# Graph attention on one core: two slots of layer 0 per loop pass, scores in one burst, PSUM banks shared out anew

## The chip, the cores and the metric

The kernel runs on one core of a Trainium2 chip. The metric is device time in microseconds from the first to the last instruction of a launch, with what little lies around it; the shown figure is the median of three runs. Engines are named as the profile names them: PE (TensorE, matrix products; PEld its weight loads), DVE (VectorE), ACT (ScalarE), POOL (GpSimd) and SP (SyncE, which issues most transfers). Products land in PSUM[...].

## The reference

Input is `x` (8 batches, 2048 nodes, 256 features) and a symmetric 0/1 matrix `adj` (2048 x 2048) with ones on the diagonal. Layer 0 is masked attention with 4 heads of 64, with a softmax of its own over every chunk of 256 keys; the chunks' contexts are added up.

```python
scores = jnp.einsum('bhnd,bhjcd->bhnjc', q, kc) / jnp.sqrt(64)
scores = jnp.clip(scores, -10.0, 10.0)
scores = jnp.where(mask == 0, -10.0, scores)
attn = jax.nn.softmax(scores, axis=-1)              # over the 256 keys of a chunk
ctx = jnp.einsum('bhnjc,bhjcd->bhnd', attn, vc)     # summed over the 8 chunks
out = layernorm(ctx @ Wo.T + bo + x) * gamma + beta
x = layernorm(x + out)
```

Layer 1 is a graph attention on the result:

```python
Wh = (x @ W)                                        # 4 heads of 64
e = leaky_relu(s_src[i] + s_dst[j], 0.2), -inf where adj == 0
alpha = softmax(e over j);  h = elu(alpha @ Wh)
x = layernorm(x + h)
```

All of it is float32.

## The kernel before

Layer 0 of a batch runs as 64 slots. A slot is one block of 512 query nodes (`q`, four of them), one pair of heads (`hp`, two) and one chunk of 256 keys (`c`, eight); 16 slots make a group, one block of queries. `scores` (L367) computes for a slot two tiles of 128 keys by 2 heads by 512 queries. Each tile takes two PSUM banks from `two_banks` (L102), which alternates between two such pairs. DVE clips each tile against a mask slab and writes it to SBUF as `pr` (L388, 1024 elements per partition); ACT takes the exponential in place (L400). `product` (L402), once per head, multiplies 512 queries' weights with the values and a column of ones (32 records of a 64-wide weight), and ACT copies the result from the one bank `pc` of the pool `psC` to `raw` (L419). `normalize` (L421) takes DVE's reciprocal of the sums (L427), and POOL scales and adds up (L434, L436).

Layer 1 of the batch before runs beside it. Its work is 192 tiles per batch: 12 units (4 heads for each of three blocks of 6, 5 and 5 tiles of 128 nodes), 16 tiles of source nodes each. `make` (L699) lets DVE form a tile `e` of edge weights (L712, 768 or 640 elements per partition; four buffers), `use` (L723) multiplies it into one bank `pa` that stays open over the unit's 16 tiles (L732). The pool `psL` has two such banks, so the next unit can begin in the other. `close` (L749) is a generator that finishes a unit in steps, one step at each call of `rest`: reciprocals of the sums read from the bank, scaling on ACT, exponential and relu, and the sum into `h1`.

Every engine runs its queue in program order; the order below is written out by hand. In slot `s` the loop of L901 emits: the slab load of slot s+3; the reciprocal of slot s-1; the scores and clips of slot s+1; the step of other work that belongs to this slot; the first product of slot s; the exponentials of slot s+1; three tiles of layer 1 (`lower.step`); the second product of slot s; and other work behind it. Three tiles of layer 1 are made ahead at the start of a batch.

The other work is kept in tables by slot number within a group. `BESIDE` holds DVE's parts of finishing the previous group (output bias, sums, statistics of the layer norms, a transpose), `BEHIND` and `AFTER` those of PE and ACT (output product, values of layer 1); small PSUM tiles for them come from one bank of the pool `psM`. In the first group of batches 2 to 7 there is no previous group, and `CLOSING` has the final norm of layer 1 of batch b-2 instead. Batch 0 has no layer 1 beside it. In its slots `masks.step` (L210) turns the matrix `adj` into the stored slabs and edges instead: a PE transpose, a DVE pass and an ACT copy per piece, through `psL`. Without layer 1 the second product of a slot uses `psL`, so that the two products have a bank each; the last batch's final slots, which have no layer 1 either (`LATE`), use the one bank. Between batches stand the projections of the next batch and the last group's steps. After batch 7 layer 1 runs alone.

PSUM in all: two pairs for `two_banks`, one bank `psC`, two `psL`, one `psM`.

Of the kernel before, what the change touches and what calls it, by code (L numbers as in the profile page):

```python
# [22 lines left out]
def adj_resnorm_kernel(  # L23
# [45 lines left out]
    LATE = 14  # L69
    WIDE = max(BANKS)  # L70
    JG = 4
    assert TILES == STEP * SLOTS and NT % JG == 0

    consts = ctx.enter_context(tc.tile_pool(name="consts", bufs=1))
    big = ctx.enter_context(tc.tile_pool(name="big", bufs=1))
    prp = ctx.enter_context(tc.tile_pool(name="prp", bufs=4))
    ep = ctx.enter_context(tc.tile_pool(name="ep", bufs=4))
    slabs = ctx.enter_context(tc.tile_pool(name="slabs", bufs=4))
    edges = ctx.enter_context(tc.tile_pool(name="edges", bufs=3))
# [4 lines left out]
    psL = ctx.enter_context(tc.tile_pool(name="psL", bufs=2, space=bass.MemoryType.PSUM))  # L84
    psM = ctx.enter_context(tc.tile_pool(name="psM", bufs=1, space=bass.MemoryType.PSUM))
# [16 lines left out]
    def two_banks(shape, name):  # L102

        turn_of[0] ^= 1
        return psA.tile(shape, F32, tag=f"psA{turn_of[0]}", name=name)
# [57 lines left out]
    def finish_constants():  # L163
        for k, a_sb in enumerate(aa):
            for c in range(KC):
                wa = small.tile([P, F], F32, tag="ee", name="wa")
                nc.vector.tensor_mul(wa, w1_sb[:, c, :F], a_sb)
                nc.vector.tensor_reduce(
                    w1_sb[:, c, F + k * H : F + (k + 1) * H],
                    wa.rearrange("p (h d) -> p h d", h=H),  # L170
                    AX.X,
                    ALU.add,
                )


        pb0 = psM.tile([P, CH], F32, tag="psM", name="pb0")
        for c in range(KC):
            nc.tensor.matmul(
                pb0[:, :F],
                lhsT=bv_sb[:, c : c + 1].to_broadcast([P, P]),  # L180
                rhs=wo_sb[:, c, :],
                start=(c == 0),
                stop=(c == KC - 1),
            )
        nc.vector.scalar_tensor_tensor(
            bo_sb, pb0[:, :F], float(NK), bo_sb, op0=ALU.mult, op1=ALU.add
        )

        nc.vector.tensor_sub(beta_sb, beta_sb, bo_sb)

# [8 lines left out]
    class Masks:  # L199
# [34 lines left out]
        def turn(self, t, m, ab):  # L234
            n, j0 = BANKS[m], FIRST[m]
            pm = psL.tile([P, WIDE, P], BF16, tag="psL", name="pm")
# [61 lines left out]
    def project(b, g):  # L298
# [14 lines left out]
        def linear(dst, w, bias, apart=False):  # L313
            if apart:
                pps = [psL.tile([P, CH], F32, tag="psL", name="pp") for _ in range(KC)]
            else:
                pp = two_banks([P, KC, CH], "pp")
                pps = [pp[:, c, :] for c in range(KC)]
            for c in range(KC):
                for kc in range(KC):  # L320
                    nc.tensor.matmul(  # L321
                        pps[c],
                        lhsT=w[:, kc, c * P : (c + 1) * P],
                        rhs=st["xT"][:, kc, :],
                        start=(kc == 0),
                        stop=(kc == KC - 1),
                    )
            for c in range(KC):
                nc.scalar.activation(  # L329
                    dst[:, c, cols], pps[c], AF.Identity, bias=bias[:, c : c + 1]  # L330
                )

        def values():
# [20 lines left out]
            lambda: linear(qT, wq_sb, bq_sb, b > 0 and g == NCH - 1),  # L354
# [11 lines left out]

    def scores(s):  # L367
        q, hp, c = where[s]
        slab = slab_of.pop(s)
        cols = slice(q * CH, (q + 1) * CH)  # L370
        pss = []
        for u in range(KT):
# [11 lines left out]
            pss.append(ps)  # L384
        probs[s] = []
# [70 lines left out]
    def context(q, hp):  # L456
        acc = accs.pop((q, hp))
        pt = psM.tile([P, CH], F32, tag="psM", name="pt")
# [42 lines left out]
    class Between:  # L501
# [3 lines left out]
        def __init__(self, b, g, sd, waug):  # L505
            self.b, self.g, self.sd, self.waug = b, g, sd, waug
            self.r = load_x(b, g, "xg")
            self.y = blocks.tile([P, QT, F], F32, tag="y", name="y")
# [9 lines left out]
        def output(self, us):  # L518
# [3 lines left out]
            else:  # L522
                po = psM.tile([P, 2, F], F32, tag="psM", name="po")
# [39 lines left out]
        def values(self, us):  # L563
            n, t = len(us), QT * self.g + us[0]
            if n == 1:
                pw = psM.tile([P, 1, CH], F32, tag="psM", name="pw")
# [22 lines left out]
    AHEAD = {12: lambda o: o.load()}  # L589
    BESIDE = {  # L590
        1: [lambda o: o.bias()],
        4: [lambda o: o.add((0, 1))],
        5: [lambda o: o.add((2, 3)), lambda o: o.a.stats((0, 1))],
# [4 lines left out]
        14: [lambda o: o.turn()],  # L598
    }
    BEHIND = {  # L600
        3: lambda o: o.output((0, 1)),
        4: lambda o: o.output((2, 3)),
        7: lambda o: o.a.apply(o.y),
        11: lambda o: o.finish(),
        14: lambda o: o.values((0,)),
        15: lambda o: o.values((1,)),
    }

    BESIDE_0 = {i: steps for i, steps in BESIDE.items() if i != 14} | {15: BESIDE[14]}
    BEHIND_0 = {i: step for i, step in BEHIND.items() if i != 14} | {15: BEHIND[14]}  # L610
    AFTER_0 = {i: lambda o, i=i: o.values((i + 1,)) for i in range(3)}
    AFTER = {0: lambda o: o.values((2,)), 1: lambda o: o.values((3,))}

    def factors(b, sd, waug):
# [10 lines left out]
        def most():  # L625
            nc.vector.tensor_reduce(top, d, AX.X, ALU.max)
            pt = psM.tile([P, CH], F32, tag="psM", name="pt")
# [4 lines left out]
        def spread():  # L632
            pb = psM.tile([P, CH], F32, tag="psM", name="pb")
# [16 lines left out]
        def rows():  # L650

            pr = psM.tile([P, CH], F32, tag="psM", name="pr1")
# [15 lines left out]
    class Layer1:  # L668
# [54 lines left out]
        def use(self):  # L723
# [17 lines left out]
            if j == NT - 1:  # L741
                self.tail.append(self.close(n, self.pa))

# [5 lines left out]
        def close(self, u, pa):  # L749
            m, h = UNITS[u]  # L750
            n = BANKS[m]
            pav = pa[:, : n * D1].rearrange("p (k d) -> p k d", k=n)

            dn = small.tile([P, n, 1], F32, tag="dn", name="dn")
            nc.vector.tensor_scalar(dn, pav[:, :, D:D1], 1e-30, None, ALU.max)  # L755
            nc.vector.reciprocal(dn, dn)  # L756
            yield 1
            hh = small.tile([P, n, D], F32, tag="hh", name="hh")
            for k in range(n):
                nc.scalar.activation(hh[:, k, :], pav[:, k, :D], AF.Copy, scale=dn[:, k, :])  # L760
# [3 lines left out]
            nc.scalar.activation(ee, hh, AF.Exp)  # L764
            hp = small.tile([P, n, D], F32, tag="hp", name="hp")
            nc.scalar.activation(hp, hh, AF.Relu)  # L766
# [8 lines left out]
            )  # L775

# [6 lines left out]
    class Close:  # L783
# [12 lines left out]
        def finish(self):  # L796
            o = blocks.tile([P, QT, F], F32, tag="y", name="o")
            self.n.apply(o)
            outgoing.append(lambda: nc.sync.dma_start(out=by_node(out, self.b, self.g), in_=o))
# [26 lines left out]
    for g in range(NCH):  # L826
# [10 lines left out]
        masks.step()  # L837
        if g == 1:
# [9 lines left out]
        3: [(1, "add"), (2, "load")],  # L848
        4: [(1, "stats")],
# [13 lines left out]
        4: [(0, "finish"), (2, "load")],  # L863
        5: [(1, "finish"), (3, "load")],
# [19 lines left out]
    for b in range(B):  # L884
        waug = blocks.tile([P, NT, H, D1], F32, tag="waug", name="waug")
        sd = small.tile([P, 2 * H, NT], F32, tag="sd", name="sd", bufs=1)
        if b == 0:
            for s in range(3):
                load_slab(s)
            scores(0)  # L890
            for u in range(KT):
                exps(0, u)
        if lower:
            for _ in range(STEP):
# [5 lines left out]
        beside, behind, after = (BESIDE, BEHIND, AFTER) if b else (BESIDE_0, BEHIND_0, AFTER_0)  # L900
        for s in range(SLOTS):  # L901
            q, hp, c = where[s]
            i = s % QS
            send()
            if s + 3 < SLOTS:
                load_slab(s + 3)
            if i == 0:
                before = group
                group = Between(b, q - 1, sd, waug) if q else None
            if i == 1 and q:  # L910
# [3 lines left out]
            if group and i in AHEAD:  # L914
                AHEAD[i](group)
            if s == SLOTS - 3 and b + 1 < B:
                turns = [project(b + 1, g) for g in range(NCH)]
                turns[0].pop(0)()
            if s:
                normalize(s - 1)  # L920
            if s + 1 < SLOTS:
                scores(s + 1)

            if s == SLOTS - 1 and b + 1 < B:
                turns[0].pop(0)()
            if i == 3 and q:
                turn_context(q - 1, 1)
            if i == QS // 2 + 3:
                turn_context(q, 0)
            if group:  # L930
                for step in beside.get(i, ()):
                    step(group)
            elif closing:
                closing.do(s, behind=False)
            product(s, 0, not lower)
            if s + 1 < SLOTS:
                for u in range(KT):
                    exps(s + 1, u)
            if lower:
                if b + 1 < B or s < SLOTS - LATE:  # L940
                    lower.step()
            elif masks.left():
                masks.step()
            product(s, 1, not lower)

            if before and i in after:
                after[i](before)
            if i == 0 and q:
                send_context(b, q - 1, 1)
            if i == QS // 2:  # L950
                send_context(b, q, 0)
            if group and i in behind:
                behind[i](group)
            elif closing and not q:
                closing.do(s, beside=False)
# [6 lines left out]
        every = tuple(range(QT))  # L962
# [20 lines left out]
        if b + 1 < B:  # L983
            (k0, v0, q0), (l1, t1, k1, v1, q1), (l2, t2, k2, v2, q2), (l3, t3, k3, v3, q3) = turns
            rest = [lambda: lower.rest(1)] if lower else []
            first = [] if b else [lambda: before.values((1,))]
            order = [begin, *rest, l1, *rest, *first, lambda: before.values((2, 3))]
            order += [*rest, ctx, *rest, k0]
            order += [steps[0], t1, steps[1], v0, steps[2], steps[3], l2, k1, steps[4], q0]
            order += [steps[5], v1, t2, l3, steps[6], q1, steps[7], k2, steps[8], steps[9], t3, v2]  # L990
            order += [lambda: [load_slab(s) for s in range(3)], fs[0], q2, fs[1], k3, fs[2], v3]
            order += [lambda: scores(0), q3, lambda: [exps(0, u) for u in range(KT)]]
        else:
# [5 lines left out]
            order += [step, lambda: lower.rest(4)]  # L999
# [62 lines left out]
```

## Time and profile before

| | us |
|---|---|
| three runs, median | 3833.12 (3832.3 to 3833.25) |
| the profiled execution | 3836.74 |
| its span, first to last instruction | 3835.0 |
| PE busy in the span | 3696.8 |
| DVE busy | 3203.6 |
| ACT busy | 1950.1 |
| slots of batch 0 (64.74 to 384.70) | 319.96 |
| 16 slots beside units of 5 tiles (2032.39 to 2133.28) | 100.89 |
| 16 slots beside units of 6 tiles (2275.93 to 2373.94) | 98.01 |
| last slot and the stretch up to the next batch's second scores (2207.09 to 2270.07) | 62.98 |

A line of instructions in order of time gives the start, the time from the first start to the last end of a run of equal instructions, the engine, the line of the kernel, the operation, what it writes and reads with their shapes, the number of records, and in brackets the idle time ahead of it with what ended it. A float32 product shows as two records, each with its own weight load. The ends of products are modelled, so what PE spends on a run of products is better read from one start to the next. A line of a group in the page gives busy time and mean length in ns, then the idle time of the engine just before. The rows for stretches of time give the length, busy time and records of PE, PEld, DVE, ACT and POOL, then clock, DMA share and GB/s.

### The profile page before, as it was taken

To read this page: it belongs to the slowest core of one execution; us is meant where nothing else is said; L and a number is where in the kernel's file an instruction comes from. 1 tells how busy PE (TensorE), PEld (TensorE's weight loads), DVE (VectorE), ACT (ScalarE), POOL (GpSimd) and SP (SyncE) were. 2 spreads that over 40 slices of the span, in tenths; PEclk is the share of its full clock that TensorE was granted. 3 is DMA by queue.
4 is the path that set the end of the run, shared out by engine and by line. 5 is a ranking of instruction groups with operands and counts; after the bars stand their busy time and mean duration, and the time that the engine had idled before them with its cause. 6 is when DMAs were issued, how large, how long until landed. Compare 5 with 4: busy or idle time off the path is not lost. (4 is left out here: it accounts for less than half of the span.)

```text
span 3835.0 us, 160246 instructions
## 1 busy us (share of the span) xinstructions
PE 3696.8 (96%) x72100; PEld 2752.3 (72%) x72100; DVE 3203.6 (84%) x4810; ACT 1950.1 (51%) x3601; POOL 1385.1 (36%) x1202
## 2 busy tenths in 40 slices
PE   9999999999999999999999999999999999999787
PEld 5656677776777777776777767777677777776676
DVE  5876499986999789995999959998699978998798
ACT  4666345555555555554555545555455555555321
POOL 1445233333433343343433324333343434334310
PEclk9999999999999999999999999999999999999999
DMA  6652333333333433333433334333333433333354
GB/s 161 151 113 65 77 101 99 96 87 112 105 95 102 91 117 101 97 101 87 131 99 92 98 92 134 97 95 88 110 110 94 104 86 118 104 99 86 93 149 123
DMA packets 756545, 398.50 MB, mean 104 GB/s; under 512 B 425744, under 2 KB 721040, under 8 KB 755856
## 3 DMA queue, kind: packets, MB, share of 16 engines
q1 hardware_dynamic: 705856, 354.54, 36.3%
q10 hardware_dynamic: 50000, 33.70, 2.7%
q8 instruction: 564, 9.24, 1.0%
q14 instruction: 125, 1.02, 0.1%
HBM read 331.22 MB, written 56.89 MB: 101 GB/s over the span
## 5 line engine op out<-in xcount | busy, mean ns | idle before, releaser
L388 DVE SCALAR_TENSOR_TENSOR pr<-ps,slab 128x1024 f32<-128x1024 f32 x1024 | 1192.5, 1205 | 215.7 <-PE ps L377 211.4
L712 DVE SCALAR_TENSOR_TENSOR e<-srow,gd,et 128x640 f32<-128x640 f32 (+1 forms) x1536 | 1349.1, 934 | 11.2 <-DMA srow<-rowD 5.7
L412 PEld LDWEIGHTS pc<-vaug,pr 128*64 128x64 f32 x32768 | 1040.6, 138 | 442.7 <-issue 253.7
L412 PE MATMUL pc<-vaug,pr 128*64 128x65 f32 x32768 | 1158.4, 224 | 40.9 <-ACT raw L419 32.0
L400 ACT ACTIVATE pr<-pr 128x1024 f32<-128x1024 f32 x1024 | 1050.4, 1057 | 158.1 <-DVE pr L388 143.6
L732 PE MATMUL pa<-waug,e 128*64 128x65 f32 x32768 | 1083.2, 224 | 41.1 <-DVE e L712 39.6
L732 PEld LDWEIGHTS pa<-waug,e 128*64 128x64 f32 x32768 | 1020.8, 139 | 67.7 <-DVE e L712 39.2
L377 PE MATMUL ps<-qT,kT 64*128 64x512 f32 x4096 | 1029.0, 619 | 3.6 <-DVE pr L388 2.6
L434 POOL TENSOR_TENSOR part<-raw,rd 128x512 f32<-128x512 f32 x448 | 467.9, 1044 | 1462.9 <-DVE rd L427 1450.4
L419 ACT COPY raw<-pc 128x260 f32<-128x260 f32 x1024 | 384.9, 377 | 1181.6 <-PE pc L412 1159.0
L377 PEld LDWEIGHTS ps<-qT,kT 64*128 64x128 f32 x4096 | 350.9, 186 | 330.7 <-issue 205.1
L436 POOL TENSOR_TENSOR acc<-acc,part 128x512 f32<-128x512 f32 x448 | 574.2, 1282 | 35.2
L427 DVE RECIPROCAL rd<-raw 128x8 f32<-128x8 f32 x512 | 100.9, 197 | 117.0 <-ACT raw L419 113.2
L434 POOL TENSOR_TENSOR acc<-raw,rd 128x512 f32<-128x512 f32 x64 | 66.8, 1043 | 336.9 <-DVE rd L427 336.1
L760 ACT ACTIVATE hh<-pa,dn 128x64 f32<-128x64 f32 x512 | 114.6, 320 | 100.6 <-DVE dn L756 96.8
L571 PE MATMUL pw<-w_sb,x1T 128*128 128x264 f32 x512 | 142.4, 415 | 8.6 <-DVE x1T L283 8.0
L487 POOL TENSOR_TENSOR rs_c<-rs_c,nhalf 128x4 f32<-128x4 f32 x32 | 55.6, 1737 | 228.4 <-DVE off_c L486 228.4
L321 PE MATMUL pp<-xT,wk_sb 128*128 128x512 f32 x256 | 119.0, 608 | 7.9 <-ACT qT L329 6.6
L527 PE MATMUL po<-wo_sb,qT 128*128 128x256 f32 x512 | 125.0, 389 | 1.1 <-DVE qT L454 0.8
L321 PE MATMUL pp<-xT,wq_sb 128*128 128x512 f32 x256 | 116.2, 596 | 0.0
L337 PE MATMUL pv<-wv_sb,xT 128*128 128x256 f32 x512 | 115.9, 379 | 0.0
L571 PEld LDWEIGHTS pw<-w_sb,x1T 128*128 128x128 f32 x512 | 93.5, 195 | 30.5 <-DVE x1T L283 8.7
(93 smaller groups left out, 1854.8 us busy)
## 6 DMA issues: line engine op xcount, KB each, us to landing
et<-edgeD SPq DMA_DIRECT2D x256, 320.0 KB, 3.1
slab<-clipD SPq DMA_DIRECT2D x512, 128.0 KB, 3.5
et<-edgeD SPq DMA_DIRECT2D x128, 384.0 KB, 3.5
srow<-rowD SPq DMA_DIRECT2D x64, 320.0 KB, 4.4
xg<-in_x_dram SPq DMA_DIRECT2D x32, 512.0 KB, 4.7
x1D<-y ACTq DMA_DIRECT2D x32, 512.0 KB, 3.0
x1g<-x1D SPq DMA_DIRECT2D x32, 512.0 KB, 5.6
out_dram<-o SPq DMA_DIRECT2D x32, 512.0 KB, 3.9
```

The source lines that it names most:

```text
L321: nc.tensor.matmul(pps[c], lhsT=w[:, kc, c * P : (c + 1) * P], rhs=st["xT"][:, kc, :], start=(kc == 0), stop=(kc == KC - 1),)
L377: nc.tensor.matmul(ps[:, k, :], lhsT=kT[rows, hp, t * P : (t + 1) * P], rhs=qT[rows, hp, cols], start=True, stop=True,)
L388: nc.vector.scalar_tensor_tensor(pr, pss[u], -CLIP, slab[:, u, :].unsqueeze(1).to_broadcast([P, 2, CH]), op0=ALU.max, op1=ALU.min,)
L400: nc.scalar.activation(pr, pr, AF.Exp, scale=0.125)
L412: nc.tensor.matmul(pc[z * D : (z + 1) * D, i, :], lhsT=probs[s][u][:, k, i * P + z * D : i * P + (z + 1) * D], rhs=vaug[:, KT * c + u, 2 * ...
L419: nc.scalar.copy(raws[s][:, k], pc)
L434: nc.gpsimd.tensor_mul(part, raw[:, :, :, :D], rd.to_broadcast([P, 2, QT, D]))
L436: nc.gpsimd.tensor_add(accv, accv, part)
L527: nc.tensor.matmul(po[:, k, :], lhsT=qT[:, c, t * P : (t + 1) * P], rhs=wo_sb[:, c, :], start=(c == 0), stop=(c == KC - 1),)
L571: nc.tensor.matmul(pw[:, k, : F + 2 * H], lhsT=self.x1T[:, c, u * P : (u + 1) * P], rhs=w1_sb[:, c, :], start=(c == 0), stop=(c == KC - 1),)
L712: nc.vector.scalar_tensor_tensor(e[:, :w], self.rows[n][:, :w], self.gd[:, h, j : j + 1], self.edge[k // JG][:, j % JG, :w], op0=ALU.max, ...
L732: nc.tensor.matmul(self.pa[z * D : (z + 1) * D, i * D1 : (i + 1) * D1], lhsT=e[:, i * P + z * D : i * P + (z + 1) * D], rhs=self.waug[:, j ...
```

## The change

The loop takes two slots at a time. Scores of slots s+2 and s+3 (four tiles, 16 records) go in one run, and only slot s+2 is clipped at once; `scores` and `clip` are now two functions. Then come four products with layer 1 between them in three parts of two tiles (`part`): the first follows the first product, the second the second product, the third the third product. Tiles are made four, none and two at a time in the three parts, and two are made ahead at the start of a batch. Slot s+3 is clipped after the second part and the reciprocal of slot s.

`two_banks` goes round three pairs of banks; `psM` is gone, its tiles come from `two_banks`; `psL` has one bank. `close` begins at once with an ACT copy of the whole bank to SBUF, and the rest works from that copy. The transposes of the masks use `two_banks` too. The output product of a group and the values are done four and two blocks at a time. Edges are loaded two tiles at a time in four buffers instead of four in three, and the loads of slabs run four and five slots ahead. `pr` has six buffers, the final output is written in place of the loaded block, and the last 16 slots of the last batch have no layer 1 (14 before), with two more steps of it in the stretch after them.

```diff
-    LATE = 14
+    LATE = 16
-    JG = 4
+    JG = 2
+    PART = 2
-    prp = ctx.enter_context(tc.tile_pool(name="prp", bufs=4))
+    prp = ctx.enter_context(tc.tile_pool(name="prp", bufs=6))
-    edges = ctx.enter_context(tc.tile_pool(name="edges", bufs=3))
+    edges = ctx.enter_context(tc.tile_pool(name="edges", bufs=4))
-    psL = ctx.enter_context(tc.tile_pool(name="psL", bufs=2, space=bass.MemoryType.PSUM))
-    psM = ctx.enter_context(tc.tile_pool(name="psM", bufs=1, space=bass.MemoryType.PSUM))
+    psL = ctx.enter_context(tc.tile_pool(name="psL", bufs=1, space=bass.MemoryType.PSUM))
...
-        turn_of[0] ^= 1
-        return psA.tile(shape, F32, tag=f"psA{turn_of[0]}", name=name)
+        turn_of[0] = (turn_of[0] + 1) % 3
+        return psA.tile(shape, dtype, tag=f"psA{turn_of[0]}", name=name)
...
-            pm = psL.tile([P, WIDE, P], BF16, tag="psL", name="pm")
+            pm = two_banks([P, WIDE, P], "pm", BF16)
...
+        scored[s] = pss
+
+    def clip(s):
+        pss, slab = scored.pop(s), slab_of.pop(s)
         probs[s] = []
         for u in range(KT):
             pr = prp.tile([P, 2, CH], F32, tag="pr", name="pr")
...
-    AHEAD = {12: lambda o: o.load()}
+    FIRST_OF = {4: lambda o: o.add(every)}
     BESIDE = {
         1: [lambda o: o.bias()],
-        4: [lambda o: o.add((0, 1))],
-        5: [lambda o: o.add((2, 3)), lambda o: o.a.stats((0, 1))],
+        5: [lambda o: o.a.stats((0, 1))],
         6: [lambda o: o.a.stats((2, 3)), lambda o: o.shift()],
         8: [lambda o: o.scale()],
         9: [lambda o: o.again(), lambda o: o.b2.stats((0, 1))],
         10: [lambda o: o.b2.stats((2, 3))],
-        14: [lambda o: o.turn()],
+        15: [lambda o: o.turn()],
     }
     BEHIND = {
-        3: lambda o: o.output((0, 1)),
-        4: lambda o: o.output((2, 3)),
+        3: lambda o: o.output(every),
         7: lambda o: o.a.apply(o.y),
         11: lambda o: o.finish(),
-        14: lambda o: o.values((0,)),
-        15: lambda o: o.values((1,)),
+        13: lambda o: o.load(),
+        15: lambda o: o.values((0, 1)),
     }
-    AFTER = {0: lambda o: o.values((2,)), 1: lambda o: o.values((3,))}
+    AFTER = {1: lambda o: o.values((2, 3))}
...
                 self.tail.append(self.close(n, self.pa))
+                next(self.tail[-1])
...
-            pav = pa[:, : n * D1].rearrange("p (k d) -> p k d", k=n)
+            hh = small.tile([P, n, D1], F32, tag="hh", name="hh")
+            nc.scalar.copy(hh, pa[:, : n * D1].rearrange("p (k d) -> p k d", k=n))
+            yield 1
...
+        def part(self, ahead):
+            self.rest(1)
+            for k in range(max(ahead, 1)):
+                if k < ahead:
+                    for _ in range(PART):
+                        self.make()
+                if k == 0:
+                    for _ in range(PART):
+                        self.use()
...
-        for s in range(SLOTS):
+        for s in range(0, SLOTS, 2):
...
+            if s:
+                normalize(s - 1)
+            if group and i in FIRST_OF:
+                FIRST_OF[i](group)
...
+            if more:
+                scores(s + 2)
+                scores(s + 3)
+                clip(s + 2)
+            elif b + 1 < B:
+                turns[0].pop(0)()
+            others(s)
+            product(s, 0, alone)
+            if more:
+                for u in range(KT):
+                    exps(s + 2, u)
+            layer1(2)
+            product(s, 1, alone)
...
+            if not lower:
+                normalize(s)
+                if more:
+                    clip(s + 3)
+                others(s + 1)
+            layer1(0)
+            if lower:
+                normalize(s)
+                if more:
+                    clip(s + 3)
+                others(s + 1)
+            product(s + 1, 0, alone)
+            if more:
+                for u in range(KT):
+                    exps(s + 3, u)
+            layer1(1)
+            product(s + 1, 1, alone)
```

In the new loop `others(s)` runs the step of `BESIDE` or `CLOSING` that belongs to slot s, `layer1` calls `part` (or, in batch 0, `masks.step` in the first and third part), and `BEHIND` and `AFTER` of both slots follow the fourth product.

## The prediction

> **What bounds the kernel now.** I read the page's engine shares first, then the busy time of three stages, then the order of instructions inside one slot. The page:
>
> ```profile
> PE 3696.8 (96%) x72100; PEld 2752.3 (72%) x72100; DVE 3203.6 (84%) x4810; ACT 1950.1 (51%) x3601; POOL 1385.1 (36%) x1202
> ...
> L388 DVE SCALAR_TENSOR_TENSOR pr<-ps,slab 128x1024 f32<-128x1024 f32 x1024 | 1192.5, 1205 | 215.7 <-PE ps L377 211.4
> ...
> L377 PE MATMUL ps<-qT,kT 64*128 64x512 f32 x4096 | 1029.0, 619 | 3.6 <-DVE pr L388 2.6
> ```
>
> The stages: all slots of batch 0 (no layer 1 yet), one group of 16 slots with layer 1 on units of 5 tiles, one on units of 6 (columns: length, then busy PE, PEld, DVE, ACT, POOL, clock, DMA):
>
> ```profile
> 64.74:384.70 319.96, 303.74 (x4835) 196.58 (x4837) 237.98 (x350) 208.66 (x331) 144.22 (x128) 0.97 0.49 111
> 2032.39:2133.28 100.89, 99.76 (x2145) 75.99 (x2145) 91.64 (x135) 53.45 (x101) 39.15 (x34) 1.00 0.38 99
> 2275.93:2373.94 98.01, 97.44 (x2306) 76.23 (x2305) 96.92 (x147) 57.24 (x98) 43.40 (x36) 1.00 0.43 129
> ```
>
> With layer 1, PE is the bound, but VectorE (DVE) has only 9 of 101 us to spare in one group and 1 of 98 in the other. It can be late without harm only as long as PE has other work to go on with. One quiet slot (start, length):
>
> ```profile
> 2038.07 1.99 PE L377 MATMUL ps<-qT,kT 64*128 64x512 f32 x8
> ...
> 2039.25 2.36 DVE L388 SCALAR_TENSOR_TENSOR pr<-ps,slab 128x1024 f32<-128x1024 f32 x2
> ...
> 2039.99 1.15 PE L412 MATMUL pc<-vaug,pr 128*64 128x65 f32 x32
> ...
> 2040.97 1.92 PE L732 MATMUL pa<-waug,e 128*64 128x65 f32 x60
> ...
> 2041.24 0.38 ACT L419 COPY raw<-pc 128x260 f32<-128x260 f32 x1 [2.42 <-PE pc L412]
> ...
> 2041.52 2.01 ACT L400 ACTIVATE pr<-pr 128x1024 f32<-128x1024 f32 x2
> ...
> 2042.72 1.10 PE L412 MATMUL pc<-vaug,pr 128*64 128x65 f32 x32
> ```
>
> Start to start: scores 1.92, product 0.98, layer 1 1.75, product 1.03 (the next begins at 2043.76), 5.68 in all. Layer 1's 60 records cost 29.2 ns each, so a product of 32 is 0.93. The score weights come in twos 0.43 apart (2038.61, 2039.04), so the scores themselves are 4 x 0.43 = 1.71. What is left, 0.21 + 0.05 + 0.10 = 0.36 us, is spent at the changes between scores and products. In batch 0 a slot runs differently:
>
> ```profile
> 180.37 0.20 DVE L427 RECIPROCAL rd<-raw 128x8 f32<-128x8 f32 x1 [0.70 <-ACT raw L419]
> ...
> 180.50 2.34 DVE L388 SCALAR_TENSOR_TENSOR pr<-ps,slab 128x1024 f32<-128x1024 f32 x2
> ...
> 181.73 2.19 ACT L400 ACTIVATE pr<-pr 128x1024 f32<-128x1024 f32 x2 [1.18 <-DVE pr L388]
> ...
> 183.83 0.68 ACT L242 CAST edge<-pm 128x640 uint8<-128x640 bf16 x1
> ...
> 184.40 0.38 ACT L419 COPY raw<-pc 128x260 f32<-128x260 f32 x1
> ...
> 184.88 0.20 DVE L427 RECIPROCAL rd<-raw 128x8 f32<-128x8 f32 x1 [0.92 <-ACT raw L419]
> ```
>
> Here a loop from reciprocal to reciprocal, not PE, sets 4.51: clips, second exponential, mask copy, copy of the product. Without masks it gives 3.93, PE's own time.
>
> **What the Trainium skill says.** "TensorEngine Tiling (Array Packing)", Key Properties: changing the tiling mode drains TensorE. The trace agrees in kind: 0.36 us per slot at two changes. "PSUM — Partial Sum Buffer", Engine vs sequencer instructions: ScalarE and VectorE queues are strict FIFO and matmuls start and complete in order. The trace agrees: the copy at 2041.24 precedes the exponentials that were ready earlier. "Perfetto Trace Analysis", Optimization Strategy: repeating bubbles on the engine that should be full can mean too few PSUM buffers. The slots above show none; the change makes a case for it.
>
> **The change, part by part.**
> *Mode changes.* Two slots share one entry and one exit: 2 x 5.68 - 0.36 = 11.01 us on PE for a quiet pair. With units of 6, layer 1 has 72 records instead of 60 per slot (+0.35 each): 11.71. Output and values in fewer bursts: per group two outputs of 1.93 and four values of 1.09 (8.2) become 3.6 + 2 x 1.97 = 7.6.
> *Three pairs of banks for four score tiles.* The fourth tile takes the first one's pair, so it waits for the first clip of its own burst. Call the burst's start 0. The first clip can start at 1.18 (2039.25 - 2038.07) and ends 1.2 later, at 2.38; the fourth tile's weights are due at 2.57. So a clip later than 1.33 stops PE for as long as it is late. Before, a late clip could be covered by a product, layer 1 and a product (3.8 us).
> *How late is the clip?* I laid out a quiet pair in the new order, unit of 5. PE: product 3.63, layer 1 4.61, product 5.78, layer 1 6.71, product 7.88, layer 1 8.81, product 9.98, end 11.01. ACT: a copy starts 1.25 after its product (4.88), the exponentials 0.28 after it and hold ACT for 1.9; second copy 7.06; reciprocal 0.48 later, 7.55. DVE after that: 0.11, two clips 2.27, two layer-1 tiles at 0.79, reciprocal 0.11: next clip at 11.63, 0.62 into the next burst. It is ready before the scores are, with 0.71 to spare. Other DVE work behind the second clips costs what exceeds 0.71; work behind the first clips has another 0.77 of its own, because there the reciprocal waits for ACT anyway. For units of 6 these are 0.94 and 0.43. PE work at a pair's end (values, output) covers DVE's.
> Group on units of 5, from the rows (vector passes 1.15, two rows' statistics 0.87): steps 6 cost 0.7, steps 8 and 9 (1.35, then 2.02) 1.9, the rest 0.7: 3.3. Closing group on units of 6 (add 1.15, statistics 1.93): 1.7 + 0.2 + 0.6 + 0.2 + 0.6 + 0.9 + 0.6 = 4.7.
> *One bank for layer 1.* At each unit's end ACT copies it out. 16 tiles are 8 parts, so ends fall on each of a pair's three parts in turn. After the first part the copy stands behind two exponentials (ready 7.5, PE due 6.71: 0.85), and the five scalings (1.1) and later passes (0.7) hold ACT before copies that PE and DVE want: 1.8 in all. After the second, the scalings delay a copy that the third product's bank needs: 0.7. After the third 0.1. That is 2.6 per 8 pairs.
> *Sum with layer 1.* Group of 5: 8 x 11.01 + 7.6 + 3.3 + 2.6 = 101.6 against 100.9, +0.7. Closing group: 8 x 11.71 + 4.7 + 2.6 = 101.0 against 98.0, +3.0. Batch 1's first group, with no closing, 0.
> *Batch 0.* The loop gets longer. From a reciprocal at 0: clip 0.11 to 1.31, the fourth tile 1.35, product 2.41, copy 3.66, exponentials 3.94, mask copy 5.85, copy 6.45, reciprocal 6.94; the other half stays 4.5. A pair is 11.4 with masks and 10.2 without (before 9.0 and 7.9). There are 18 and 14 of them: 349; other work on the loop (output and values ahead of a burst, the sum before the first clip) 22. So 371 against 320: +51.
> *Last batch.* Its last 16 slots have no layer 1: 8 x 10.2 + 6 = 88 against 81, and two more layer-1 steps (about 2.5 each, DVE's time for three tiles) go into the end: +12.
> *At nothing:* smaller edge loads (3.1 us to landing, asked for at least four tiles ahead), output in place, the tables' shifts, the stretches between batches (63 us, PE 61 busy in both orders). If the edge loads came late, each would cost under 1 us; -5 to +15 for all of these.
> Total: 51 + 20 x 0.7 + 6 x 3.0 + 12 = +95, less a few where two stalls of a pair overlap: +92. The profiled execution was 3836.74 (span 3835.0), 3.6 above the median of 3833.12; on the median, 3925. The unseen costs: PE's saving per pair 0.25 to 0.36; stalls with layer 1 between 0 (DVE's lateness is never met) and twice my sum.
>
> **Rivals.**
> *The mode changes win.* If DVE is never later than the fourth tile, 216 pairs keep 0.36 each (-77) and the joined bursts -12; with +51 and +12 that is 3807. It decides as soon as new stalls with layer 1 stay under some 18 us, 0.08 a pair. For it: PE is 96% busy. Against: DVE's 97 of 98 us. 15%.
> *No slack at all.* If quiet pairs also wait for the first clip, because the copy before the reciprocal is later than I have it, another 0.5 a pair: +108, 4030. 20%.
> *Batch 0 keeps its time* because its product gets ahead of the fourth tile: 3874. The program order speaks against it. 10%.
> *Gains and losses cancel*, within 0.2%: 5%. My forecast 50%.
>
> **How the numbers follow.** About 0.2%, 8 us, is what can be told from no change. Faster is the first rival, 0.15; same 0.05; slower the rest, 0.80. The range, 3835 to 4020, leaves out the first rival and part of the second.
>
> **What would show it.** In the changed profile: score bursts of 16 records in which the fourth tile's weights wait for L392 in busy pairs; quiet pairs at 11.0; batch 0's slots near 370 us; layer 1's first part after a unit waiting for L752. Wrong if batch 0's stage stays at 320, or if pairs with statistics also run at 11.0.

## The result and the profile after

| | before | after | after / before |
|---|---|---|---|
| median, us (4 runs each) | 3832.71 (3830.84 to 3833.25) | 3967.40 (3965.39 to 3970.28) | 1.0353 [1.0335, 1.0371] |
| span of the profiled execution | 3835.0 | 3965.5 | |

The kernel became slower by about 135 us. The page after, in the same three lines:

```profile
PE 3658.4 (92%) x72100; PEld 2769.0 (70%) x72100; DVE 3233.0 (82%) x4786; ACT 1967.2 (50%) x3617; POOL 1392.6 (35%) x1202
...
L392 DVE SCALAR_TENSOR_TENSOR pr<-ps,slab 128x1024 f32<-128x1024 f32 x1024 | 1193.5, 1206 | 129.3 <-PE ps L377 123.6
...
L377 PE MATMUL ps<-qT,kT 64*128 64x512 f32 x4096 | 1004.9, 619 | 99.4 <-DVE pr L392 96.3
```

PE's busy time fell by 38 us, and yet the span grew by 130: PE now stands idle. The clip itself is as long as before (1206 ns against 1205). What is new is the last line: the scores waited 96.3 us for the clips, where before it was 2.6.

Where the 130.5 us lie is read by splitting both traces at the same instructions: the first scores of each batch after its projections, and the last reciprocal of layer 0.

| stretch | before, us | after, us | difference | forecast |
|---|---|---|---|---|
| start to the first scores | 60.7 | 64.6 | +4.0 | 0 |
| batch 0: first scores to batch 1 | 387.6 | 438.3 | +50.7 | +51 |
| of it: the loop, first scores in it to its last product's end | 321.4 | 378.8 | +57.4 | +51 |
| of it: from there to batch 1's first scores | 62.1 | 53.5 | -8.6 | 0 |
| batch 1 | 455.1 | 458.0 | +2.9 | +2.1 |
| batches 2 to 6, each | 455.7 | 463.8 | +8.1 | +5.1 |
| batch 7 and the end | 653.2 | 685.5 | +32.2 | +16.4 |
| of it: last 16 slots | 83.1 | 82.0 | -1.1 | +7 |
| of it: last reciprocal of layer 0 to the end | 264.2 | 285.4 | +21.2 | +5 |

The forecast column regroups the sum's own terms: three groups on units of 5 in batch 1; the same and a closing group in batches 2 to 6; two groups, a closing group and the last batch's 12 in batch 7. In the table of times before, the stretch of 62.98 us ends at the next batch's first scores, not at its second.

First, a busy pair with layer 1, in order of time:

```profile
2165.11 1.21 DVE L551 TENSOR_TENSOR y<-y,xg 128x1024 f32<-128x1024 f32 x1
2165.64 2.85 PE L377 MATMUL ps<-qT,kT 64*128 64x512 f32 x12
...
2166.36 0.75 DVE L481 BATCH_NORM_STATS2 st_b<-y 128x6 f32<-128x256 f32 x2
...
2167.24 1.67 DVE L710 SCALAR_TENSOR_TENSOR e<-srow,gd,et 128x640 f32<-128x640 f32 x2
2168.83 0.20 DVE L431 RECIPROCAL rd<-raw 128x8 f32<-128x8 f32 x1
2168.94 2.31 DVE L392 SCALAR_TENSOR_TENSOR pr<-ps,slab 128x1024 f32<-128x1024 f32 x2
...
2170.18 1.13 PE L377 MATMUL ps<-qT,kT 64*128 64x512 f32 x4 [1.70 <-DVE pr L392]
```

Three tiles of the burst (12 records) run at once. The fourth (the next four records) stands for 1.70 us, until the first clip, begun at 2168.94, has freed its pair of banks. DVE is late because vector passes and two layer-1 tiles stood ahead of the reciprocal. In the group 2116.18 to 2217.76 (101.58 us, forecast 101.6) the quiet pair takes 11.02 us (forecast 11.01), while the pairs that follow step 6, and steps 8 and 9, take 11.5 and 13.85.

Second, batch 0, where the loop through the clip sets the pace:

```profile
84.99 0.20 DVE L431 RECIPROCAL rd<-raw 128x8 f32<-128x8 f32 x1 [0.82 <-ACT raw L423]
...
86.35 1.13 PE L377 MATMUL ps<-qT,kT 64*128 64x512 f32 x4 [0.23 <-DVE pr L392]
...
87.41 1.15 PE L416 MATMUL pc<-vaug,pr 128*64 128x65 f32 x32
...
88.66 0.38 ACT L423 COPY raw<-pc 128x260 f32<-128x260 f32 x1 [3.71 <-PE pc L416]
...
90.84 0.79 ACT L245 CAST edge<-pm 128x768 uint8<-128x768 bf16 x1
...
92.00 0.20 DVE L431 RECIPROCAL rd<-raw 128x8 f32<-128x8 f32 x1 [1.61 <-ACT raw L423]
```

Reciprocal, clip, fourth score tile, product, copy, exponentials, mask copy, copy, reciprocal: 7.01 us for this half of the pair, 6.94 in the forecast. A pair without masks takes 10.25 (forecast 10.2). Pairs with masks take more than the forecast's 11.4: the eight of the first group 12.2 on average. Mask transposes now take their banks from the same round as the scores, and each second one of a pair waits for a clip:

```profile
93.38 0.44 PE L241 MATMUL pm<-identb,ab 128*128 128x128 bf16 x5 [2.37 <-DVE pr L392]
```

Over the loop of batch 0 (64 to 450 us) these waits are longer in total than those of the fourth score tile (total, times, longest):

```profile
PE pm L241 <- DVE pr L392: 39.6, 17, 2.4
PE ps L377 <- DVE pr L392: 17.8, 17, 2.2
```

The forecast had no such wait. The stretch behind the loop got shorter, in part because the next values hardly wait for their transposed block any more, before and after:

```profile
390.87 2.13 PE L571 MATMUL pw<-w_sb,x1T 128*128 128x264 f32 x4 [4.73 <-DVE x1T L283]
```

```profile
449.78 0.49 PE L575 MATMUL pw<-w_sb,x1T 128*128 128x264 f32 x1 [0.35 <-DVE x1T L286]
```

Third, the end of a unit. The next unit's first product waits for ACT's copy of the one bank:

```profile
2174.67 0.42 ACT L752 COPY hh<-pa 128x325 f32<-128x325 f32 x1
...
2175.14 1.39 PE L730 MATMUL pa<-waug,e 128*64 128x65 f32 x40 [0.65 <-ACT hh L752]
```

Two things came out larger. The first pair of a closing group begins with this:

```profile
2362.42 1.94 DVE L710 SCALAR_TENSOR_TENSOR e<-srow,gd,et 128x768 f32<-128x768 f32 x2
...
2364.27 2.35 DVE L392 SCALAR_TENSOR_TENSOR pr<-ps,slab 128x1024 f32<-128x1024 f32 x2
...
2365.55 1.13 PE L377 MATMUL ps<-qT,kT 64*128 64x512 f32 x4 [1.86 <-DVE pr L392]
```

Nothing covers the start of a batch: the clips of slot 1 and two tiles made ahead stand before the clip, so PE stops for 1.86 us. This closing group takes 104.1 us (2360.79 to 2464.86), where the forecast had 101.0. The six closing groups take 103.7 to 107.6 us, before 97.6 to 98.4. In batch 7 the first pair is another 2.8 longer.

And the end. Rows of stretches from the last reciprocal of layer 0, after and before (length, then busy PE, PEld, DVE, ACT, POOL):

```profile
3680.15:3965.50 285.35, 212.51 (x5120) 187.29 (x5120) 254.49 (x407) 67.19 (x185) 37.89 (x29) 0.89 0.42 122
```

```profile
3570.77:3835.00 264.23, 205.43 (x4995) 177.71 (x4993) 243.24 (x398) 56.93 (x165) 36.04 (x27) 0.93 0.44 126
```

DVE is the bound here, busy 254 of 285 us. Its busy time grew by 11.2 and its idle time by 9.9. One part shows in the list of DVE's waits there, which had no such line before, and one in the order of time (DVE tiles and POOL's scaling of the values; then the same place before):

```profile
DVE e L710 <- DMA et<-edgeD: 7.9, 5, 2.7
```

```profile
3730.38 11.53 DVE L710 SCALAR_TENSOR_TENSOR e<-srow,gd,et 128x640 f32<-128x640 f32 x6
...
3731.37 9.87 POOL L657 TENSOR_TENSOR waug<-waug,ed 128x1024 f32<-128x1024 f32 x4
```

```profile
3619.94 4.15 DVE L712 SCALAR_TENSOR_TENSOR e<-srow,gd,et 128x640 f32<-128x640 f32 x3
```

Three undisturbed tiles take 2.44 us (at 3727.11), 0.81 each. Beside POOL six take 11.53 instead of 4.9; before, only three fell there and took 4.15 instead of 2.4. That is about 5 us more; six more tiles in the stretch are another 5, and the late edges 7.9 in this execution.

### The profile page after: what moved, and what is told of

The parts are those of the page before. It is cut to its first block, busy times and chain, and to the rows that moved or that the text cites. A ratio compares the mean times of both kernels' runs of the same rounds, so it can differ in the third digit from the quotient of the medians.

```text
span 3965.5 us, 161239 instructions
## 1 busy us (share of the span) xinstructions
PE 3658.4 (92%) x72100; PEld 2769.0 (70%) x72100; DVE 3233.0 (82%) x4786; ACT 1967.2 (50%) x3617; POOL 1392.6 (35%) x1202
## 5 line engine op out<-in xcount | busy, mean ns | idle before, releaser
L710 DVE SCALAR_TENSOR_TENSOR e<-srow,gd,et 128x640 f32<-128x640 f32 (+1 forms) x1536 | 1363.0, 938 | 20.7 <-PE pa L730 8.9
L392 DVE SCALAR_TENSOR_TENSOR pr<-ps,slab 128x1024 f32<-128x1024 f32 x1024 | 1193.5, 1206 | 129.3 <-PE ps L377 123.6
L730 PE MATMUL pa<-waug,e 128*64 128x65 f32 x32768 | 1129.8, 225 | 81.5 <-DVE e L710 48.8
L730 PEld LDWEIGHTS pa<-waug,e 128*64 128x64 f32 x32768 | 1045.6, 140 | 113.8 <-DVE e L710 51.7
L377 PE MATMUL ps<-qT,kT 64*128 64x512 f32 x4096 | 1004.9, 619 | 99.4 <-DVE pr L392 96.3
L377 PEld LDWEIGHTS ps<-qT,kT 64*128 64x128 f32 x4096 | 365.2, 189 | 565.4 <-DVE pr L392 281.3
L440 POOL TENSOR_TENSOR acc<-acc,part 128x512 f32<-128x512 f32 x448 | 575.2, 1284 | 35.2
L760 ACT ACTIVATE hh<-hh,dn 128x64 f32<-128x64 f32 x512 | 132.2, 337 | 22.2 <-DVE dn L757 20.1
L575 PE MATMUL pw<-w_sb,x1T 128*128 128x264 f32 x512 | 128.4, 399 | 5.0 <-DVE x1T L286 3.3
L752 ACT COPY hh<-pa 128x325 f32<-128x325 f32 (+1 forms) x96 | 42.7, 445 | 147.6 <-PE pa L730 147.6
```

The source lines that it names most:

```text
L377: nc.tensor.matmul(ps[:, k, :], lhsT=kT[rows, hp, t * P : (t + 1) * P], rhs=qT[rows, hp, cols], start=True, stop=True,)
L392: nc.vector.scalar_tensor_tensor(pr, pss[u], -CLIP, slab[:, u, :].unsqueeze(1).to_broadcast([P, 2, CH]), op0=ALU.max, op1=ALU.min,)
L440: nc.gpsimd.tensor_add(accv, accv, part)
L575: nc.tensor.matmul(pw[:, k, : F + 2 * H], lhsT=self.x1T[:, c, u * P : (u + 1) * P], rhs=w1_sb[:, c, :], start=(c == 0), stop=(c == KC - 1),)
L710: nc.vector.scalar_tensor_tensor(e[:, :w], self.rows[n][:, :w], self.gd[:, h, j : j + 1], self.edge[k // JG][:, j % JG, :w], op0=ALU.max, ...
L730: nc.tensor.matmul(self.pa[z * D : (z + 1) * D, i * D1 : (i + 1) * D1], lhsT=e[:, i * P + z * D : i * P + (z + 1) * D], rhs=self.waug[:, j ...
```

## The experiments

Each changes the changed kernel, unless it is said otherwise. All ratios are against the kernel before.

**The clip ahead of the reciprocal.** If the burst loses by DVE's queue order, then moving the reciprocal behind the clip should help.

```diff
-            if s:
-                normalize(s - 1)
...
                 clip(s + 2)
+            if s:
+                normalize(s - 1)
             others(s)
```

> The changed kernel with one edit: the reciprocal of slot s-1 stands behind the two clips of slot s+2 instead of ahead of them. Theory (in batch 0 the loop runs from the copy of the last product over the reciprocal and the first clip to the fourth score tile): the first clip no longer waits for that copy; a pair of batch 0 falls from 12 to about 11 with masks and from 10.25 to about 8.6 without, so batch 0 with the stretch behind it goes from 438 to about 400, the last batch's bare slots gain a few us, quiet pairs with layer 1 stay at 11.0; total about 3915. Rival (the burst itself, in its place ahead of the first product, holds the loop, whatever stands ahead of the clip): batch 0 stays within 10 us of 438, total within 15 us of 3967.

Measured: 4110.35 us, ratio 1.0723 [1.0707, 1.0738]. In batch 0 the loop theory holds for pairs without masks, which fall from 10.25 to 8.6 us. The stage falls only from 438.3 to 425.2, not to 400: PE's waits for the clips at score tiles fall from 17.8 to 7.5 us, but those of the mask transposes stay (39.5). The batches with layer 1 lengthen by about 24 us each, which neither theory had foreseen. Here is the order of time:

```profile
2097.06 5.31 DVE L710 SCALAR_TENSOR_TENSOR e<-srow,gd,et 128x768 f32<-128x768 f32 x4
2097.29 1.65 POOL L438 TENSOR_TENSOR part<-raw,rd 128x512 f32<-128x512 f32 x1 [7.42 <-DVE rd L431]
2099.01 1.88 POOL L440 TENSOR_TENSOR acc<-acc,part 128x512 f32<-128x512 f32 x1
```

POOL starts its two passes when the reciprocal is done. With the reciprocal moved they fall beside the layer-1 tiles, and both get longer; with the clips first in line behind the reciprocal they fell beside the clips. The groups by shape, of this kernel and then of the changed kernel:

```profile
L710 DVE SCALAR_TENSOR_TENSOR e<-srow,gd,et 128x640 f32<-128x640 f32 x1024 | 1075.8, 1105 | 7.8 <-PE pa L730 4.1 <-DMA et<-edgeD 3.4 <-PE ps L377 0.2
...
L440 POOL TENSOR_TENSOR acc<-acc,part 128x512 f32<-128x512 f32 x448 | 689.9, 1540 | 35.2
```

```profile
L710 DVE SCALAR_TENSOR_TENSOR e<-srow,gd,et 128x640 f32<-128x640 f32 x1024 | 867.1, 897 | 13.4 <-PE pa L730 7.2 <-DMA et<-edgeD 3.2
...
L440 POOL TENSOR_TENSOR acc<-acc,part 128x512 f32<-128x512 f32 x448 | 575.2, 1284 | 35.2
```

The Trainium skill, "SBUF — State Buffer", Who interferes with whom, says that a DVE instruction with two inputs from SBUF contends with a GpSimd instruction that reads SBUF, and one with at most one SBUF input doesn't. The runs agree: a tile (two inputs in SBUF) goes from 897 to 1105 ns and POOL's sum from 1284 to 1540, while the clips, which take one input from PSUM, are 1206 ns beside the same passes. That the 24 us come of this is read from PE's waits between 1000 and 3150 us: those for clips rise from 49.7 to 98.5, those for tiles from 1.7 to 30.7. No run took the contention away and kept the new order.

**The burst undone, everywhere and in batch 0 alone.**

```diff
                 scores(s + 2)
-                scores(s + 3)
                 clip(s + 2)
...
                 if more:
+                    scores(s + 3)
                     clip(s + 3)
```

> The changed kernel with the burst undone alone: scores of slot s+3 go in front of the third product instead of behind those of slot s+2; four products with layer 1 between, three pairs of banks, single banks for products and layer 1 stay. Theory (the fourth tile of the burst is what waits): PE pays 0.36 us more per pair, quiet pairs 11.37 instead of 11.02, but the pairs with statistics lose their stalls (13.85 goes to about 12), and batch 0 with the stretch behind it falls from 438 to about 385; total about 3885. Rival (the single banks and the order of the copies cost, not the burst): batch 0 stays near 430 and the groups of 16 slots rise by 0.36 x 8 from 101.6 to about 104; total about 4040.

The second kernel makes this edit only where there is no layer 1 (`if not lower`):

> The changed kernel with the burst undone in batch 0 alone. Theory: batch 0 with the stretch behind it goes from 438 to about 385 as in the run that undoes it everywhere, every other stage stays as in the changed kernel; total about 3914. Rival (batch 0 is longer because masks, scores and products share three pairs of banks): 430 or more, total above 3955.

Measured: everywhere, 3948.72 us, 1.0301 [1.0286, 1.0316]; in batch 0 alone, 3900.75, 1.0173 [1.0156, 1.019]. The stage of batch 0 falls from 438.3 to 371.9 and 371.6, 16 us under the kernel before. So the burst costs batch 0 some 67 us, and the other edits gain there. With the burst undone the mask transposes wait for no clip any more (they still share the three pairs, so the second run's rival, the sharing alone, is out). How the 67 us divide between their waits and the fourth score tile's, no run separates. With layer 1, undoing it makes each of batches 2 to 6 some 10 us *longer* (473.4), and the group of 5 takes 103.7 instead of 101.58, as the first run's rival had it. The stalls didn't go; they changed place. PE's longest waits between 1000 and 3150 us, with the burst undone and then in the changed kernel (total, times, longest):

```profile
PE pa L730 <- DVE e L710: 71.7, 61, 2.5
```

```profile
PE ps L377 <- DVE pr L392: 49.7, 57, 1.9
...
PE pa L730 <- DVE e L710: 1.7, 4, 0.4
```

DVE's lateness is met either way: with the burst at the fourth score tile, without it at layer 1's tiles.

**An edge buffer more**, and edges asked for one load earlier.

```diff
-    edges = ctx.enter_context(tc.tile_pool(name="edges", bufs=4))
+    edges = ctx.enter_context(tc.tile_pool(name="edges", bufs=5))
...
-                self.load_edge(k // JG + 2)
+                self.load_edge(k // JG + 3)
```

> The changed kernel with edges asked for three loads ahead in five buffers instead of two in four. Theory (in the end, where layer 1 runs alone, the smaller loads come late behind stores that SP waits for): the part from the last reciprocal of layer 0 to the end falls from 285 to about 272, nothing else moves; total about 3955. Rival (the end is longer because of two more steps and the copy of the bank at each unit's end): no change above 3 us.

Measured: 3962.83 us, 1.0338 [1.0323, 1.0354]. The waits of tiles for edges are gone, and the end falls from 285.4 to 276.7, by 8.7. The total fell by only 4.6; in this execution one batch's closing group was 5 us longer. How late the edges come differs between executions: in the runs above that keep the end's code, the waits are 7.9, 5.6, 6.1 and 4.1 us and the end 285.4, 282.9, 283.9 and 280.5. Less the waits it is 276 to 278 each time, so the late edges cost 4 to 8 us.

**POOL scales a unit's rows** in place of ACT, with batch 0's burst undone.

```diff
-            for k in range(n):
-                nc.scalar.activation(hh[:, k, :D], hh[:, k, :D], AF.Copy, scale=dn[:, k, :])
+            nc.gpsimd.tensor_mul(hh[:, :, :D], hh[:, :, :D], dn.to_broadcast([P, n, D]))
```

> The kernel with the burst undone in batch 0 (3901 us), with one edit: at a unit's end the five or six scalings on ACT become one POOL multiplication over the whole block. Theory (at a unit's end ACT's work holds up the copies that the next product and reciprocal wait for, 1.3 us per 8 pairs): a group of 16 slots falls from 101.6 to about 100.3, the whole to about 3870. Rival (POOL's pass falls beside VectorE's layer-1 tiles, which have two operands in SBUF, and both slow down, as in the run with the reciprocal behind the clips): groups stay within 0.3 us, total 3890 to 3910.

Measured: 3895.37 us, 1.016 [1.0145, 1.0175]; batches 2 to 6 take 462.8 us on average, with batch 0's burst undone alone 465.3, and the group of 5 falls from 101.58 to 101.3. That is the rival's range. Between 1000 and 3150 us PE's waits for ACT's copies of products fall from 10.4 to 3.8 us, but those for clips rise from 52.7 to 60.5, and the tiles of 128x640 lengthen from 899 to 922 ns. What the scalings on ACT cost by themselves is therefore not shown.

**Five vector passes left out.** These two leave out the adding of `bo`, `beta` and the block in layer 0's norms, the product with `gamma`, and the adding of `x` in layer 1's last norm: once from the changed kernel with batch 0's burst undone, once from the kernel before. The statistics stay.

```diff
-            nc.vector.tensor_add(self.r, self.r, row)
+            pass
...
-            nc.vector.tensor_mul(self.y, self.y, row)
+            pass
...
-            nc.vector.tensor_add(self.y, self.y, self.r)
...
-            nc.vector.tensor_add(self.h, self.h, self.x)
```

> The kernel with the burst undone in batch 0, with less work on VectorE: the passes that add bo and beta, multiply by gamma, add the block again, and add x in the last norm are left out. Theory (beside layer 1 the paired slots are slower only because VectorE is late for the fourth score tile): a group on units of 5 falls from 101.6 to about 99, PE's own floor being 95.7; the closing group from 104 to about 100.5; total about 3790, and about 35 above the kernel before with the same passes left out instead of 68. Rival (what is lost per group lies with the single banks and ACT): groups fall by less than 1 us and the distance to the lighter kernel before stays at 60 or more.

> The kernel before, with the same five kinds of VectorE passes left out. Theory: its groups were bound by PE and fall only from 100.9 to about 99.3; total about 3755. Rival (VectorE bounds it as well): groups fall to 98 or below.

Measured: 3822.92 us (0.9974 [0.9967, 0.998]) and 3765.69 us (0.9823 [0.9808, 0.9838]). In the changed order the group of 5 falls to 99.46 us; its pair behind steps 8 and 9 goes from 13.85 to 12.02, the one behind step 6 from 11.5 to 11.2. In the kernel before it falls to 99.13. The distance between the orders shrinks from 68 us to 57, not to the 35 expected, so most of it isn't these passes. Of the distance, 26 us lie from batch 7's first scores to the end (661.4 against 635.3). With the passes gone, three pairs of a group still take 12.25, 12.02 and 12.13 us where the quiet one takes 11.02: 3.3 us together, most of it by its place the ends of units (the pair of 12.02 keeps statistics too). DVE is still late at times: between 1000 and 3150 us the fourth score tiles wait 20.3 us, where with batch 0's burst undone alone it is 52.7.

**The added steps of layer 1 drawn forward in the end**, with batch 0's burst undone.

```diff
-fs[1], step, fs[2]]
-            order += [step, step, step, lambda: lower.rest(4)]
+fs[1], step, step, step, fs[2]]
+            order += [step, lambda: lower.rest(4)]
```

> The kernel with the burst undone in batch 0 (3901 us), with the two added steps of layer 1 after the last batch put ahead of POOL's scaling of the values instead of beside it. Theory (VectorE's layer-1 tiles and POOL's passes slow each other when both read two operands from SBUF: there six tiles took 11.5 us instead of 4.8): of the six tiles at most three stay beside POOL's passes, and the part from the last reciprocal to the end falls from 280 to about 276; total about 3897. Rival (the tiles were late because of edge loads): the same six tiles take as long in their new place, no change above 1.5 us.

Measured: 3896.76 us, 1.0172 [1.0155, 1.0189], and an end of 282.4 against 280.5 without the edit, within what the edges' lateness alone moves. It decided nothing: the same six tiles still ran beside POOL's scaling (11.53 us, as above), since their order on DVE hardly moved. What that contention costs the span was not shown by taking it away.

**The kernel before with some bursts joined.** What of the change needs no burst of scores? First the values of layer 1 two blocks at a time, in the pair of banks that the kernel has already; then the output product in one burst as well, its sum ahead of slot 4's reciprocal.

```diff
-        14: lambda o: o.values((0,)),
-        15: lambda o: o.values((1,)),
+        15: lambda o: o.values((0, 1)),
...
-    AFTER = {0: lambda o: o.values((2,)), 1: lambda o: o.values((3,))}
+    AFTER = {1: lambda o: o.values((2, 3))}
```

> The kernel before, with one part of the change alone: the values of a group in two bursts of two blocks, in the pairs of banks of the scores, instead of four single ones through the small bank. Theory (each change between kinds of product costs PE 0.2 us): 0.4 us less per group with layer 1, some us less in batch 0; total about 3820. Rival (a value tile in a score pair makes the next scores wait): groups lengthen by 0.5 us or more; total above 3840.

> The kernel before with joined values alone, beside the one above on the same chip: about 3827, as before.

> The kernel before with both joined bursts and nothing else of the change: the values in two bursts of two blocks, and the output product of a group in one burst of four, its sum ahead of the slot's clips. Theory: one more change between kinds of product less per group, 0.2 us, 21 to 24 times: about 5 us below the kernel with joined values (3827), so about 3822. Rival (the output tile holds one of only two score pairs until VectorE has added it, and the next scores wait): groups lengthen by 0.5 us or more each, total 3835 or more.

Measured: the values joined, 3826.68 us, 0.9984 [0.9977, 0.9991], and again 3826.64, 0.9987 [0.998, 0.9993]; the output as well, 3824.88, 0.9981 [0.9973, 0.9988]. Values slots of 6.77 us each (four of them) become 7.66 and 5.68, twice. This beats both kernels by a little, about 6 us over the one before; the joined output can't be told apart from it.

## Why the prediction was right and where it was off

**Right: the direction and its mechanism.** The fourth score tile waits for the first clip wherever DVE is late, and quiet pairs keep the saving: 11.02 us. The group of 5 was right to the tenth, and so nearly were its parts: the three pairs with output and values take 7.8 us more than quiet ones (put at 7.6), the four others 5.6 (put at 5.9). Steps 8 and 9 were put at 1.9 us, and taking their two vector passes out gave 1.83 back. Step 6 was put at 0.7; taking its one pass out gave 0.3, its statistics remaining. The total was not as good: +92 was forecast and 135 measured, most of the rest in the closing groups and in the end.

**Batch 0: the loop right, the sum in part by luck.** The loop ran as laid out (7.01 against 6.94 us, 10.25 against 10.2), and undoing the burst there gave 67 us back. But that +50.7 meets +51 hides two terms that were left out and nearly cancel. The loop as a whole took 378.8 us where 371 was put, without the mask transposes' waits; the stretch behind, put at nothing, fell by 8.6. That the stage falls under the kernel before with the burst undone, so that the burst alone costs more than the difference, was not in the sum either.

**Off: the last batch and the end.** "+12" was 7 for bare slots and 5 for two more steps. The last 16 slots were not slower: 82.0 us, before 83.1 (two of the 16 had layer 1 then). The end grew by 21.2, of which the sum had the 5. The step that failed is the one put "at nothing": the edge loads. It had each late load under 1 us; DVE waited 7.9 us for five, 4 to 8 from one execution to another, and one more buffer took these waits away. The rest of the end, some 7 to 8 us, is by the trace mostly the six tiles beside POOL's scaling (about 5); that is argued from durations, and no run took it away.

**Off: closing groups,** +6.1 in the one shown, where +3.0 was put, and up to +9 in batch 7. The stretches between batches were also "at nothing", and from batch 1 on their length hardly changes (last product to the next first scores 52.4 us, after 51.4); but the first pair behind them has no earlier work to cover the fourth tile's wait, 1.86 us. This wait could have been laid out with the same rule as the others. The rest has no one place that I could name. Some of it is PE standing idle where the trace names no cause ("issue"), here 0.76 us in the middle of layer 1's products at 2451.03. Such waits come to 13.0 us between 1000 and 3150 us, where the list of the kernel before has none; why stays open.

**Off inside the right sum of the group of 5.** The forecast put the loss with layer 1 on the burst and a gain of 0.36 us per pair against it. The burst undone showed that this is not how the parts divide: the group gets 2.1 us longer, and DVE's lateness stops PE at layer 1's tiles instead. Beside layer 1, with the other edits in place, the burst is a gain. What the change loses there, against the kernel before, must come with those other edits: with the burst undone, batches 2 to 6 are still 17.7 us longer each. Two candidates show in the traces: unit ends, up to 3.3 us per eight pairs (2.6 in the forecast), and layer-1 tiles made just in time, for which PE waits 71.7 us once the burst is undone. No run gave layer 1 its second bank or its third tile ahead back, so which takes how much is not shown. DVE's work itself hardly grew (3233.0 us busy, before 3203.6, and 11 of these 29 us lie in the end).

The rivals: "the mode changes win" needs stalls below 0.08 us a pair, and the fourth tile alone stalled 49.7 us between 1000 and 3150, some 0.3 a pair. "No slack at all" fails on the quiet pair, "batch 0 keeps its time" on the stage.

## What to carry to other kernels

When products are gathered into a burst, ask of its last tile which buffer it takes and who frees it; a burst one tile longer than the free buffers puts the consumer's queue order on PE's path, and where that consumer is part of a loop, as in batch 0, the price is paid in every pass. Count whoever else takes buffers from the same round: here the mask transposes waited longer than the burst's own last tile. Check the cover at the start of each stage by itself, and count late loads in the stage that has the least to do besides. Gather what already has a free buffer, and leave the rest.

## What was not expected of the hardware

DVE and POOL slow each other when DVE takes both inputs from SBUF while POOL reads it: the place of one reciprocal of 0.2 us decided whether POOL's passes ran beside PSUM-reading clips (no loss) or beside layer-1 tiles (897 to 1105 ns, and POOL 1284 to 1540). The run with the reciprocal moved lost about 24 us per batch. With POOL's larger passes of 128x1024 beside them six tiles took 11.53 us, more than double.
